# A transformer decoder layer on one core: the first attention fetch moved between queues, and the FFN's inner layernorm root computed by Newton's method on GpSimd

## The chip, the cores and the metric

The kernel runs on one core of a Trainium2 chip. The metric is the device time of one execution in microseconds (us); less is better. PE is TensorE, DVE is VectorE, ACT is ScalarE, POOL is GpSimd and SP is SyncE, which here only issues DMAs. PE, ACT, SP and POOL each have a queue in which instructions stand in order.

## The reference

One pre-norm decoder layer in fp32 for 4 batches of 1024 tokens with 256 features and 16 heads of 16 features, a context of 64 tokens, and an FFN of width 1024:

```
def _layernorm(x, eps=1e-05):
    return (x - mean(x)) / sqrt(var(x) + eps)

x = x + attn(_layernorm(x))            # softmax(q k^T) / 16 @ v, out projection
x = x + xattn(_layernorm(x), ctx)      # softmax(q k^T / 4) @ v over 64 context tokens
h = _layernorm(x) @ ternary(W_fc).T    # 256 -> 1024
h = gelu(h)
h = (h - mean(h)) * rsqrt(var(h) + 1e-05) * ln_w + ln_b      # the inner layernorm, over 1024
x = x + h @ ternary(W_proj).T          # 1024 -> 256
```

`ternary(W)` rounds W over its mean absolute value to -1, 0 or 1.

## The kernel before, in words

**Front, 0 to 63 us.** The first layernorm and the q and k projections of batch 0 run tile by tile. `project` (lines 360 to 376) computes two feature blocks of q or k for 512 tokens on PE into a bank of `ps_ring` (seven banks in turn), ACT copies it, rounded, to the first half of `hl` (line 370), DVE writes the remainder to its second half (line 371), and one DMA stores both to DRAM in `kept_q` or `kept_k` (line 376). Of the first feature block, the first store goes out on SP and the other three on ACT's queue. `fetch(u)` (lines 379 to 410) then brings the q and k of one group of four heads back into SBUF as small DMAs of 16 rows each, which lay the high and low parts of each head beside one another. A group has two pairs of heads, `pair` 0 and 1, and each pair two sides `n`, on partitions from 64n. Group 0 is fetched in halves of 512 columns so that it can start early: for each pair first q (first columns, line 401), then k (first and second columns, line 404), and at the end the second columns of q. Of k, the pieces of side `n` = 0 go out on ACT's queue and those of `n` = 1 on SP's.

**Groups, 63 to 1095 us.** There are 16 groups `u` (4 batches x 4 groups of 4 heads), each of 16 steps. Each step computes scores, their exponentials on ACT (line 909) and the weighted sum of values in `ps_acc`; meanwhile scores of the following half group go through PE once more and DVE takes their maxima `mx` (`maxima`, line 447), 32 for a half group of group 0 at the beginning. `turn_maxima` makes the negative maximum `nm` of them (line 456), without which the exponentials can't start. The order of all matmuls on PE is the order of the program. The other stages (next batch's projections, out projection, cross attention) are put between steps by credit lines.

**Tail, 1095 to 1355 us.** The FFN runs in eight halves of a batch, i = 0 to 7, each of four tiles of 128 tokens. `widen(i)` normalises x (line 265), transposes it on PE, writes it rounded to `xh` (ACT, line 279) with its remainder in `xl` (DVE, line 281), multiplies by `wfc`, takes Gelu (ACT, line 1029) and the statistics `mvh` of each tile (DVE, lines 1032 and 1033). It then takes the root through `ln_rstd` (lines 245 to 248): Sqrt on ACT into `sd`, reciprocal on DVE into `rsh`, then `nmr` = -mean * rsh on DVE (line 1037). With these the four tiles of h are normalised, two on DVE (line 1040), two on ACT (line 1043). `narrow(i)` transposes h on PE, writes it times `lnw` as `hT` (ACT, line 1063) with remainder `hl` (DVE, line 1064), and multiplies both by `wproj`; at the end x is completed and stored. Sqrt, Exp and Gelu lie in different activation tables of ACT, and a change between them is an ACT_TABLE_LOAD.

Each of the two is a generator, and the `yield`s cut it into pieces. A loop takes the next piece of whichever generator has the smallest place in a table:

```
WIDE, NARROW = (-6, -4, 0, 1, 3, 7, 8, 10, 12), (2, 4, 5, 6, 9, 11, 13, 14, 15)
wides = [Source(widen(i), 16 * i, WIDE) for i in range(halves)]
narrows = [Source(narrow(i), 16 * (i + 1), NARROW) for i in range(halves)]
```

So `narrow(i)` runs beside `widen(i + 1)`. In turns with `turn % 5 in (0, 2)` the loop takes a piece of the last batch's out projection and cross attention instead, as long as there are any; that work uses Exp (line 636). A piece of `widen` whose tag is Gelu or Sqrt is held back (`apart`) while a run of four Exp pieces is not complete. The program's order binds PE; on ACT and DVE a scheduler orders the instructions by what they need.

Of the kernel before, what the change touches and what calls it, by code (L numbers as in the profile page):

```python
# [8 lines left out]

F32 = mybir.dt.float32  # L10
F32R = mybir.dt.float32r
DRAM = bass.MemoryType.DRAM
AF = mybir.ActivationFunctionType
ALU = mybir.AluOpType
# [7 lines left out]
P = 128  # L22
NT = S // P
NG = 4
NU = B * NG
LN_EPS = 1e-5
# [4 lines left out]
def decoder_layer(ctx, tc, a, out):  # L31
# [15 lines left out]
    nc = tc.nc  # L47
# [54 lines left out]
    for name in ("wq", "wk"):  # L102
# [5 lines left out]
        t = const.tile([P, E // P, H, D], F32, name=name)  # L108
# [4 lines left out]
    for name in ("bq", "bk"):  # L113

        t = const.tile([P, 2], F32, name=f"{name}_c")
# [33 lines left out]
    own = post_pool.tile([P, 4], F32, name="own")  # L149
    sel_x = post_pool.tile([P, 8, SK], F32R, name="sel_x")  # L150

# [9 lines left out]
    for i in range(3):  # L161
        t = (const if i else main).tile([P, NT, VW], F32, tag=f"v_sb{i}", name=f"v_sb{i}")
# [81 lines left out]
    def ln_rstd(pool, rs, mv):  # L244
        n = mv.shape[1]
        sd = pool.tile([P, n], F32, tag="sd", name="sd", bufs=2)
        nc.scalar.activation(sd, mv[:, :, 1], AF.Sqrt, bias=eps_t[:, 0:1])
        pinned(nc.vector.reciprocal(out=rs, in_=sd))

    def ln_normalised(pool, mv, rs, i, t, n):  # L250
        xn = pool.tile([P, n, E], F32, tag="xn", name="xn", bufs=2)
        if state["split"]:
            nmr = pool.tile([P, n], F32, tag="nmr", name="nmr", bufs=2)
            nc.vector.scalar_tensor_tensor(
                nmr, mv[:, i : i + n, 0], -1.0, rs[:, i : i + n], ALU.mult, ALU.mult
            )
            for k in range(n):
                nc.scalar.activation(  # L258
                    xn[:, k, :], xs(t + k)[:, 0, :], AF.Identity, bias=nmr[:, k : k + 1],
                    scale=rs[:, i + k : i + k + 1],  # L260
                )
            return xn
        for k in range(n):
            pinned(
                nc.vector.tensor_scalar(
                    xn[:, k, :], xs(t + k)[:, 0, :], mv[:, i + k, 0:1], rs[:, i + k : i + k + 1],
                    ALU.subtract, ALU.mult,
                )
            )
        return xn  # L270
# [81 lines left out]
    def project(b, c):  # L352
# [6 lines left out]
        for side, half in ((0, 0), (1, 0), (1, 1), (0, 1)):  # L359
# [3 lines left out]
            for i0 in range(0, 512, width):  # L363
# [5 lines left out]
                )  # L369
                nc.scalar.activation(hl[:, 0, part].bitcast(F32R), pq, AF.Identity, bias=bias)  # L370
                nc.vector.scalar_tensor_tensor(  # L371
# [7 lines left out]
    def fetch(u):  # L379

        b, g = divmod(u, NG)
        pairs = qk_of[u] = []
        rest = []
        for pair in range(2):
            q = main.tile([P, S], F32R, tag="q", name="q", bufs=4)
            k = main.tile([P, S], F32R, tag="k", name="k", bufs=4)
            pairs.append((q, k))
            kept_q, kept_k = split_of[b, g // 2]
            f0 = 64 * (g % 2) + 32 * pair

            def parts(t, kept, order, n, cols, issue, f0=f0):
                for i, part in enumerate(order):
                    r, f = 64 * n + 16 * i, f0 + 16 * n
                    issue(out=t[r : r + 16, cols].bitcast(F32), in_=kept[part, f : f + 16, cols])

            if u:
                halves = (slice(0, S),)
            else:
                halves = (slice(0, 512), slice(512, S))
            for n in range(2):  # L400
                parts(q, kept_q, (0, 0, 1, 1), n, halves[0], dma)
            for cols in halves:
                for n in range(2):
                    parts(k, kept_k, (0, 1, 0, 1), n, cols, dma if u or n else nc.scalar.dma_start)
            for n in range(2):
                for cols in halves[1:]:
                    rest.append((parts, q, kept_q, (0, 0, 1, 1), n, cols, dma))
            if pair:
                for f, *args in rest:
                    f(*args)  # L410
            yield
# [42 lines left out]
    def turn_maxima(u, mx):  # L454
# [3 lines left out]
        dst = nm_s[:, :, :, 0:2, :]  # L458
        nc.vector.tensor_copy(dst[:, :, :, :, 0].bitcast(F32R), by_side)
        nc.vector.tensor_tensor(dst[:, :, :, :, 1], by_side, dst[:, :, :, :, 0], ALU.subtract)  # L460
        yield
        views = turned([nm_s[:, n, :, :, :].rearrange("p n a l -> p (n a l)") for n in range(4)])
        mT = main.tile([P, 512], F32R, tag="mT", name="mT", bufs=3)
        for r, v in enumerate(views):
# [237 lines left out]
    urgent, due, later, aside = deque(), Line(), Line(), Line()  # L702
# [132 lines left out]
    first, parts = ln1(0), project(0, 0)  # L835
# [35 lines left out]
    parts = project(0, 1)  # L871
# [40 lines left out]
    for u in range(NU):  # L912
# [27 lines left out]
        for step in range(2 * NT):  # L940
            half, kb = divmod(step, NT)
# [15 lines left out]
            exps = [scores(u, half, kb, 0)]  # L957
# [42 lines left out]
    ffn = ctx.enter_context(tc.tile_pool(name="ffn", bufs=1))  # L1000
    out_view = out.rearrange("(t p) d -> p t d", p=P)
    h_of = {}
    NH = NT // 2

    def widen(i):
        t0 = i * NH
        xh = ffn.tile([P, 2, NH * P], F32R, tag="xh", name="xh", bufs=2)
        xl = ffn.tile([P, 2, NH * P], F32R, tag="xl", name="xl", bufs=2)
        for t in range(0, NH, 2):
            cols = slice(t * P, (t + 2) * P)  # L1010
            xn = ln_normalised(ffn, mv3, rs3, t0 + t, t0 + t, 2)
            ln_transposed(xh[:, :, cols], xn, rest=xl[:, :, cols])
            if t == 0:
                yield ""
        h = ffn.tile([P, NH, HID], F32, tag="h", name="h", bufs=2)
        mv = ffn.tile([P, NH, 2], F32, tag="mvh", name="mvh", bufs=2)
        rs = ffn.tile([P, NH], F32, tag="rsh", name="rsh", bufs=2)
        h_of[i] = h
        for t in range(NH):
            yield "Gelu"  # L1020
            ph = ps["wide"]()
            for half in range(2):
                for k in range(4):
                    c, part = divmod(k, 2)
                    matmul(
                        ph[:, half, :], lhsT=(xl, xh)[part][:, c, t * P : (t + 1) * P],
                        rhs=wfc[:, c, half * 512 : (half + 1) * 512], start=k == 0, stop=k == 3,
                    )
            nc.scalar.activation(h[:, t, :], ph.rearrange("p a f -> p (a f)"), AF.Gelu)  # L1029
            st = ffn.tile([P, 2, 6], F32, tag="bnh", name="bnh", bufs=3)  # L1030
            for half in range(2):
                nc.vector.bn_stats(out=st[:, half, :], in_=h[:, t, half * 512 : (half + 1) * 512])  # L1032
            nc.vector.bn_aggr(out=mv[:, t, :], in_=st)
        yield "Sqrt"
        ln_rstd(ffn, rs, mv)
        nmr = ffn.tile([P, NH], F32, tag="nmr", name="nmr", bufs=2)
        nc.vector.scalar_tensor_tensor(nmr, mv[:, :, 0], -1.0, rs, ALU.mult, ALU.mult)
        for t in range(0, NH, 2):
            yield ""
            nc.vector.tensor_scalar(  # L1040
                h[:, t, :], h[:, t, :], mv[:, t, 0:1], rs[:, t : t + 1], ALU.subtract, ALU.mult
            )
            nc.scalar.activation(
                h[:, t + 1, :], h[:, t + 1, :], AF.Identity, bias=nmr[:, t + 1 : t + 2],
                scale=rs[:, t + 1 : t + 2],
            )
# [57 lines left out]

    WIDE, NARROW = (-6, -4, 0, 1, 3, 7, 8, 10, 12), (2, 4, 5, 6, 9, 11, 13, 14, 15)
    halves = 2 * B
    wides = [Source(widen(i), 16 * i, WIDE) for i in range(halves)]
    narrows = [Source(narrow(i), 16 * (i + 1), NARROW) for i in range(halves)]  # L1110
    exps = turn = 0
    tag = later.tag
    while tag is not None or narrows:
        turn += 1
        if tag is not None and turn % 5 in (0, 2):
            exps += "Exp" in tag
            tag = next(last, None)
            continue
        sources = []
        if wides:  # L1120
            i = halves - len(wides)
            first = len(wides[0].places) <= len(WIDE) - 2
            late_x = i >= 2 * (B - 1) and tag is not None
            full = first and len(narrows) > halves + 1 - i
            apart = exps % NG and tag is not None and wides[0].tag in ("Gelu", "Sqrt")
            if not (late_x or full or apart):
                sources.append(wides[0])
        if narrows and len(narrows) > len(wides):
            sources.append(narrows[0])
        if not sources:  # L1130
            continue
        source = min(sources, key=lambda source: source.places[0])
        source.step()
        if not source:
            (wides if source in wides else narrows).pop(0)
# [58 lines left out]
```

## Time and profile before

| | |
|---|---|
| median of 3 runs | 1352.89 us (1351.7 to 1353.23) |
| profiled execution | 1356.75 us |
| its span | 1355.0 us (1.75 us of the execution lie around it) |
| mean granted TensorE clock | 0.978 of full speed |
| PE busy | 1282.8 us, 95% of the span |
| DVE, ACT, POOL busy | 75%, 66%, 4% |
| ACT table loads | 15.4 us at line 1029, 24.4 us at line 247, 11.5 us at line 909, 3.8 us at line 636, each load 1.283 us |

The profile is of one execution, 3.86 us above the median. A timeline row gives the start, the duration, the engine, the line, the operation and its tiles, how many of them were run together (x2), and in brackets how long the engine stood idle before and what ended that. An engine with a q (ACTq, SPq) is issuing a DMA. The slices of the page cut the span into 40 equal parts of 33.9 us and show the busy share of each in tenths.

### The profile page before, as it was taken

How to read it: one execution, taken by the hardware profiler on the slowest of the kernel's cores; microseconds unless marked ns; L12 is line 12 of the kernel's file. 1: busy time of each engine (PE TensorE's matmuls, PEld its weight loads, DVE VectorE, ACT ScalarE, POOL GpSimd, SP SyncE). 2: the span in 40 equal slices, each digit the busy share in tenths (PEclk: the TensorE clock that was granted, in tenths of full speed). 3: DMA queues.
4: the chain of work that ended last, by engine and by line, in shares of the span. 5: the costliest groups of instructions: out<-in, count | busy, mean ns of one | idle time of the engine just before them, and what ended most of it. 6: DMA issues, size and time to landing. Idle time of an engine off the chain costs nothing.

```text
span 1355.0 us, 27659 instructions
## 1 busy us (share of the span) xinstructions
PE 1282.8 (95%) x11000; PEld 719.0 (53%) x11000; DVE 1013.4 (75%) x2130; ACT 896.3 (66%) x1654; POOL 53.4 (4%) x66
## 2 busy tenths in 40 slices
PE   4889999999999999989999999999999999999987
PEld 2344545545545454444545544545455457776777
DVE  5777877867878888778777777778888468585765
ACT  1267686756687767677676676676766756575755
POOL 4000000003010000011000000010000000000000
PEclk9789999999999999999999999999999999999989
DMA  5440412212120202030202111312110010100000
GB/s 165 134 126 29 129 37 90 79 48 63 39 89 1 63 5 60 32 94 25 71 30 66 28 36 53 105 40 87 41 55 1 1 63 1 59 4 32 1 32 31
DMA packets 46576, 72.72 MB, mean 54 GB/s; under 512 B 11536, under 2 KB 28176, under 8 KB 46448
## 3 DMA queue, kind: packets, MB, share of 16 engines
q1 hardware_dynamic: 44976, 68.47, 16.8%
q10 hardware_dynamic: 1328, 2.10, 0.5%
q8 instruction: 87, 1.43, 0.4%
q0 software_dynamic: 144, 0.39, 0.2%
q14 instruction: 41, 0.34, 0.1%
HBM read 46.81 MB, written 24.12 MB: 52 GB/s over the span
## 4 chain that ended last, share of the span: by engine, by line
PE 74%; DVE 16%; ACT 7%; DMA 2%; issue 1%; SPq 0%; DVEq 0%; ACTq 0%
PE ps_ring L57 43%; PE ps_acc L57 15%; PE ps_wide L57 8%; DVE mx L447 7%; PE ps_misc L57 3%; DVE nm L603 3%; ACT exp L909 2%; PE ps_misc L60 2%; PE ps_ring L60 2%; ACT xn L258 1%; DVE bn L241 1%; DMA kept_k<-hl 1%; DMA x<-in_x 1%; ACT ex L636 1%; SPq L63 0%
## 5 line engine op out<-in xcount | busy, mean ns | idle before, releaser
L447 DVE TENSOR_REDUCE mx<-ps_ring 128x1 f32<-128x512 f32 x1024 | 646.9, 682 | 157.5 <-PE ps_ring L57 156.8
L909 ACT ACTIVATE exp<-ps_ring 128x512 f32<-128x512 f32 x1024 | 549.1, 607 | 182.1 <-PE ps_ring L57 178.7
L57 PE MATMUL ps_ring<-q,k 64*128 64x512 f32 x1024 | 280.4, 475 | 6.5 <-ACT exp L909 5.6
L57 PE MATMUL ps_ring<-k,q 64*128 64x512 f32 x1024 | 266.5, 428 | 18.2 <-DMA k<-kept_k 6.6
L57 PE MATMUL ps_acc<-exp,v_sb 128*32 128x512 f32 x2048 | 275.3, 610 | 0.0
L57 PE MATMUL ps_ring<-mT,sel 64*128 64x512 f32 x1024 | 233.4, 402 | 0.4 <-ACT mT L465 0.4
L57 PEld LDWEIGHTS ps_ring<-q,k 64*128 64x128 f32 x1024 | 115.8, 186 | 198.1 <-ACT exp L909 65.7
L57 PEld LDWEIGHTS ps_ring<-k,q 64*128 64x128 f32 x1024 | 127.0, 187 | 100.6 <-ACT exp L909 41.8
L57 PEld LDWEIGHTS ps_ring<-mT,sel 64*128 64x128 f32 x1024 | 108.7, 187 | 6.5 <-ACT mT L465 0.7
L57 PEld LDWEIGHTS ps_acc<-exp,v_sb 128*32 128x32 f32 x2048 | 40.5, 108 | 67.8 <-issue 66.0
L1064 DVE SCALAR_TENSOR_TENSOR hl<-ps_misc,lnw,hT 128x512 fp32r<-128x512 f32 x64 | 46.6, 734 | 20.0 <-ACT hT L1063 19.8
L1032 DVE BATCH_NORM_STATS2 bnh<-h 128x6 f32<-128x512 f32 x64 | 41.1, 680 | 24.7 <-ACT h L1029 24.6
L57 PE MATMUL ps_wide<-wfc,xl 128*128 128x512 f32 x128 | 55.6, 435 | 3.6 <-DVE xl L281 3.1
L1029 ACT ACTIVATE h<-ps_wide 128x1024 f32<-128x1024 f32 x32 | 32.7, 1025 | 36.8 <-PE ps_wide L57 36.7
L57 PE MATMUL ps_wide<-wproj,hl 128*128 128x256 f32 x256 | 46.8, 306 | 10.6 <-DVE hl L1064 10.5
L1063 ACT ACTIVATE hT<-ps_misc,lnw 128x512 fp32r<-128x512 f32 x64 | 42.9, 687 | 15.3 <-PE ps_misc L60 15.2
L57 PE MATMUL ps_wide<-wfc,xh 128*128 128x512 f32 x128 | 52.9, 413 | 0.0
L241 DVE BATCH_NORM_STATS2 bn<-x 128x6 f32<-128x256 f32 x96 | 39.0, 416 | 5.8 <-DMA x<-in_x 4.1
L57 PEld LDWEIGHTS ps_wide<-wproj,hl 128*128 128x128 f32 x256 | 35.3, 194 | 14.3 <-DVE hl L1064 12.6
L57 PE MATMUL ps_wide<-wproj,hT 128*128 128x256 f32 x256 | 42.0, 287 | 0.0
L371 DVE SCALAR_TENSOR_TENSOR hl<-ps_ring,bq_c,hl 128x256 f32<-128x256 f32 (+1 forms) x30 | 14.8, 500 | 31.0 <-ACT hl L370 31.0
L60 PE MATMUL ps_misc<-ident,h 128*128 128x128 f32 x256 | 37.3, 275 | 0.0
(167 smaller groups left out, 1424.0 us busy)
## 6 DMA issues: line engine op xcount, KB each, us to landing
q<-kept_q SPq DMA_DIRECT2D x240, 64.0 KB
k<-kept_k SPq DMA_DIRECT2D x240, 64.0 KB
kept_q<-hl SPq DMA_DIRECT2D x15, 512.0 KB
kept_k<-hl SPq DMA_DIRECT2D x14, 512.0 KB
out<-x SPq DMA_DIRECT2D x16, 256.0 KB
x<-in_x SPq DMA_DIRECT2D x3, 1024.0 KB
x_kept<-x SPq DMA_DIRECT2D x3, 1024.0 KB
x<-x_kept SPq DMA_DIRECT2D x3, 1024.0 KB
```

The lines of the kernel that those rows point to most:

```text
L57: ordered(nc.tensor.matmul(*args, **kwargs))
L60: ordered(nc.tensor.transpose(*args))
L241: pinned(nc.vector.bn_stats(out=st, in_=xs(t)[:, 0, :]))
L258: nc.scalar.activation(xn[:, k, :], xs(t + k)[:, 0, :], AF.Identity, bias=nmr[:, k : k + 1], scale=rs[:, i + k : i + k + 1],)
L371: nc.vector.scalar_tensor_tensor(hl[:, 1, part], pq, bias, hl[:, 0, part], ALU.add, ALU.subtract)
L447: nc.vector.tensor_reduce(mx[:, t, 2 * pair + n : 2 * pair + n + 1, kh], pm, AX.X, ALU.max)
L603: nc.vector.tensor_reduce(nm[:, t, s, :], pm[s].rearrange("p (h k) -> p h k", k=SK), AX.X, ALU.max, negate=True,)
L909: nc.scalar.activation(ex[:, n, :], pe[n], AF.Exp)
L1029: nc.scalar.activation(h[:, t, :], ph.rearrange("p a f -> p (a f)"), AF.Gelu)
L1032: nc.vector.bn_stats(out=st[:, half, :], in_=h[:, t, half * 512 : (half + 1) * 512])
L1063: nc.scalar.activation(hT, pt, AF.Copy, scale=w)
L1064: nc.vector.scalar_tensor_tensor(hl, pt, w, hT.bitcast(F32), ALU.mult, ALU.subtract)
```

## The change

It does two things. First, `fetch(0)` issues nothing on ACT's queue any more: the k pieces of side 0 go to SP's queue for pair 0 (8 DMAs) and to GpSimd's queue for pair 1 (8 DMAs). Second, the FFN's inner layernorm takes its inverse root in `ln_root`, 17 GpSimd operations on 128x4 elements: a first value from the bits of the variance, three Newton steps, and `nmr`; the Sqrt on ACT and the reciprocal and `nmr` on DVE of this layernorm go. The yield with the tag Sqrt goes with them, so `widen` has one piece less. In the table the last two pieces of `widen`, which normalise h, stand at 12 and 13 instead of 10 and 12, and a piece of `narrow` stands at 8 that was at 13. The share of turns for the last batch goes from 2 of 5 (0.400) to 7 of 17 (0.412).

```diff
+I32 = mybir.dt.int32
...
+    def ln_root(pool, rs, mv):
+        n = mv.shape[1]
+        by = pool.tile([P, 4, n], F32, tag="root", name="root", bufs=2)
+        var, half, t, nmr = (by[:, i, :] for i in range(4))
+        engine = nc.gpsimd
+        engine.tensor_scalar(var, mv[:, :, 1], LN_EPS, None, ALU.add)
+        engine.tensor_scalar(half, var, -0.5, None, ALU.mult)
+        engine.tensor_scalar(
+            rs.bitcast(I32), var.bitcast(I32), -0.5, float(0x5F3759DF), ALU.mult, ALU.add
+        )
+        for _ in range(3):
+            engine.tensor_tensor(t, rs, half, ALU.mult)
+            engine.tensor_tensor(t, t, rs, ALU.mult)
+            engine.tensor_scalar(t, t, 1.5, None, ALU.add)
+            engine.tensor_tensor(rs, rs, t, ALU.mult)
+        engine.tensor_tensor(nmr, mv[:, :, 0], rs, ALU.mult)
+        engine.tensor_scalar(nmr, nmr, -1.0, None, ALU.mult)
+        return nmr
...
             for cols in halves:
                 for n in range(2):
-                    parts(k, kept_k, (0, 1, 0, 1), n, cols, dma if u or n else nc.scalar.dma_start)
+
+                    aside = u == 0 and pair == 1 and n == 0
+                    parts(k, kept_k, (0, 1, 0, 1), n, cols, nc.gpsimd.dma_start if aside else dma)
...
             nc.vector.bn_aggr(out=mv[:, t, :], in_=st)
-        yield "Sqrt"
-        ln_rstd(ffn, rs, mv)
-        nmr = ffn.tile([P, NH], F32, tag="nmr", name="nmr", bufs=2)
-        nc.vector.scalar_tensor_tensor(nmr, mv[:, :, 0], -1.0, rs, ALU.mult, ALU.mult)
+        nmr = ln_root(ffn, rs, mv)
...
-    WIDE, NARROW = (-6, -4, 0, 1, 3, 7, 8, 10, 12), (2, 4, 5, 6, 9, 11, 13, 14, 15)
+    WIDE, NARROW = (-6, -4, 0, 1, 3, 7, 12, 13), (2, 4, 5, 6, 8, 9, 11, 14, 15)
...
-        if tag is not None and turn % 5 in (0, 2):
+        if tag is not None and turn % 17 in (0, 2, 5, 7, 10, 12, 15):
...
-            apart = exps % NG and tag is not None and wides[0].tag in ("Gelu", "Sqrt")
+            apart = exps % NG and tag is not None and wides[0].tag == "Gelu"
```

## The prediction

> **What bounds the kernel now.** I read the page first: busy shares, slices, the chain that ended last; then the timeline of each engine where the slices are not full, and the windows there.
>
> ```profile
> span 1355.0 us, 27659 instructions
> PE 1282.8 (95%) x11000; PEld 719.0 (53%) x11000; DVE 1013.4 (75%) x2130; ACT 896.3 (66%) x1654; POOL 53.4 (4%) x66
> PE   4889999999999999989999999999999999999987
> POOL 4000000003010000011000000010000000000000
> PEclk9789999999999999999999999999999999999989
> ```
>
> PE is full except in the first three slices (34 us each) and the last two; Pool is empty. The change touches only those two ends, the attention steps between them shift as a block. So the question is how many us PE's stalls lose at each end.
>
> Front: the timeline of ACT, then of DVE, 24 to 64 us (columns: start, duration, engine, line, operation, count, idle before it).
>
> ```profile
> 25.82 2.39 ACTq L394 DMA_DIRECT2D k<-kept_k  x2
> 28.73 8.18 ACTq L394 DMA_DIRECT2D k<-kept_k  x13
> 37.01 0.84 ACT L370 ACTIVATE hl<-ps_ring,bq_c 128x256 fp32r<-128x256 f32 x2 [10.88 <-DMA q<-kept_q]
> 44.27 0.87 DVE L371 SCALAR_TENSOR_TENSOR hl<-ps_ring,bq_c,hl 128x256 f32<-128x256 f32 x2
> 45.06 0.87 DVE L371 SCALAR_TENSOR_TENSOR hl<-ps_ring,bk_c,hl 128x256 f32<-128x256 f32 x2
> 48.24 13.25 DVE L447 TENSOR_REDUCE mx<-ps_ring 128x1 f32<-128x512 f32 x22 [1.12 <-PE ps_ring L57]
> 61.52 0.19 DVE L456 TENSOR_REDUCE nm<-mx 128x16 f32<-128x32 f32 x1
> ```
>
> ACT issues the k fetches of group 0 until 36.9 us, so its four hl copies come at 37.0 instead of 26, DVE's partners of them at 44.3, and four of the seven ring banks stay taken. PE, which fills banks for the 32 maxima (mx), starves, and runs slowly too: the window 36 to 48 has a granted clock of 0.50. Only ten maxima are done before 48.24; the other 22 run back to back at 13.25/22 = 0.602 us; attention's first exponentials wait for nm at 61.5.
>
> Tail: one half of the FFN, 1284 to 1290 us, by the timeline; then the window around it (core's span, PE, PEld, DVE, ACT, POOL busy, clock).
>
> ```profile
> 1284.82 1.28 ACT L247 ACT_TABLE_LOAD   x1
> 1286.11 0.30 ACT L247 ACTIVATE sd<-mvh,eps_t 128x4 f32<-128x4 f32 x1
> 1286.44 0.18 DVE L248 RECIPROCAL rsh<-sd 128x4 f32<-128x4 f32 x1 [0.81 <-ACT sd L247]
> 1286.84 0.16 DVE L1037 SCALAR_TENSOR_TENSOR nmr<-mvh,rsh 128x4 f32<-128x4 f32 x1
> 1286.91 1.53 DVE L1040 TENSOR_SCALAR h<-h,mvh,rsh 128x1024 f32<-128x1024 f32 x2
> 1287.03 2.37 ACT L1043 ACTIVATE h<-h,nmr,rsh 128x1024 f32<-128x1024 f32 x2
> 1288.36 0.75 DVE L1064 SCALAR_TENSOR_TENSOR hl<-ps_misc,lnw,hT 128x512 fp32r<-128x512 f32 x1
> 1289.16 1.22 PE L57 MATMUL ps_wide<-wproj,hl 128*128 128x256 f32 x4 [2.70 <-DVE hl L1064]
> 1286.00:1296.00 10.00, 7.30 (x36) 6.22 (x36) 7.40 (x15) 6.22 (x8) 0.00 (x0) 0.83 0.15 52
> ```
>
> The root stands in the middle of ACT's and DVE's queues: PE waits for an hl that stands behind both normalisations. There are four such gaps: 1124.02 (2.92), 1233.50 (2.70; this one for two table loads between Exp and Gelu), 1289.16 (2.70), 1313.32 (2.90); 11.2 us, and PE then runs at half clock for 3.4 us (three times, 1.7 us lost) or 6.8 (the last, 3.4 lost), another 8.5. Gaps of up to 1.5 us (1336.77, 1263.07) are not followed by that.
>
> **Part 1: the first fetch.** In the changed program's order ACT issues no k piece; SP issues 16 k pieces after its first q pieces instead of 8, and Pool the other 8.
> - ACT's four hl follow at once: its kept_k store goes out at about 23.6 instead of 24.96 (before, it stands behind the first k issue, which waits for the first store), lands 4.03 later (24.96 to 28.99) at 27.7, and hl of both engines is done by about 27.5.
> - SP: 16 x 0.46 us (3.66/8) from 27.8 to 35.2. The first eight are the pieces needed first; they land, at 1.8 to 2.8 us, by 34.3. The second eight by 37.5. Then eight q of the second pair to 38.9, eight k to 42.6, sixteen q to 50.0. SP's old end of this is 48.7, so the stores behind it and fetch(1) come 1.3 us later; group 1's pieces, there by 70, are not used before the second half of group 0's steps (about 95), nor the x loaded behind them before 88, which hides it. If that cover were gone it would cost those 1.3.
> - Pool is idle after 20.7. Eight issues at 0.54 to 0.69 (its own rows bo, xbv) are 4.3 to 5.5 us, from about 27.8 to 33; landing at 5.7 to 6.2 (same rows) is 39. They are needed at the 17th maximum, about 44: covered by 5 us. Nothing else of Pool's is due then.
> - The maxima: from 33 us, the first eight at half clock for some 3.4 us (0.86 each) and then at 0.602, done by 40; the other 24 at 0.602 = 14.4: 54.5 to 55.5. nm comes at about 55 instead of 61.5. Gain 6.5; at an SP pace of 0.6 (the first three q have 3.69/3, with a wait in it) the first pieces land 3 us later and some 3 are left; bounds 2 and 8.
>
> **Part 2: the root on Pool.** Removed: 15 table loads (the changed order has 10 in the tail, before 25) at 1.283 = 19.2 us of ACT, 8 sd x 0.298 = 2.4, and of DVE 8 x (0.175 + 0.157) = 2.7. Neither is PE's time; it counts only through the gaps. A row says what stands behind a load: 1284.82 + 1.28 is 1286.10, and sd starts at 1286.11. The Trainium skill, "ScalarE: Activation LUTs", section "What ACT_TABLE_LOAD costs", adds a drain of about 1.38 us to each switch; that would make it 39.9 us of ACT instead of 19.2, but this trace shows no such drain.
>
> Added: 17 Pool operations of 128x4 in a chain (15 to rsh, 17 to nmr) for each half, each waiting for the one before. No 128x4 operation of Pool is in the trace. Below: memset 128x1, 0.10 us. Above: memset 64x32, 0.317. Nearest: copy 128x64 0.237 and 128x256 0.401, 0.85 ns an element, so 0.185 for four elements; two operands cost twice that per element (128x512 1.274 against 0.625), which is nothing at four. To it comes the hand-over, 0.03 to 0.05 (nm's three steps on DVE start 0.03 after one another; Pool shows 0.05). I take u = 0.23 a step, the copy row's; the bounds are 0.13 and 0.36, a step can't cost less than nothing, and the two rivals below stand just inside them, at 0.15 and 0.33. The chain is then 15u = 3.45 and 17u = 3.9 us, where load, sd, reciprocal and nmr take 2.2 (1284.82 to 1287.0), and ACT and DVE stand in order behind it: xh, xl, q and nm wait with it.
>
> Against this speaks the Trainium skill, "GPSIMD Engine Reference", section "4.1 Engine selection": elementwise work belongs on VectorE, about 2 times faster for two inputs. By a factor of two on DVE's 0.16 to 0.18 the step would be an estimated 0.34 and the change a loss; the copy row above says 0.185.
>
> Place by place, from the end of mvh's aggregation, with the durations above (normalisation DVE 1.53, ACT 2.37; xl 0.69; xh 0.57), gain of PE:
> - half 0: xl ready at 1117.55 + 15u + 1.53 + 0.69 + 0.1, against 1124.02: 4.15 - 15u.
> - half 1: q stands behind ACT's normalisation, PE would reach it 1.05 us after a root without duration: 1.05 - 17u (a new stall).
> - half 3: the Exp/Gelu gap goes (+3.1), DVE's nm of the cross attention waits behind the normalisation: 3.2 - 15u.
> - half 5 to 6: from the last wfc to the next 10.6 now (1280.45 to 1291.03), then 3.1 to mvh + 15u + 2.4: 5.1 - 15u.
> - half 6 to 7: 10.76 now, then 6.9 + 17u: 3.86 - 17u.
> - last: 7.78 now (1330.03 to 1337.81), then 5.6 + 17u, and the gap of 0.73 at 1340.02 goes: 2.9 - 17u.
> - halves 2 and 4: PE has other work; 0.
>
> Sum 20.3 - 96u. At 0.23: -1.8. Half-clock stretches: the one behind 1289.16 goes (+1.7), one comes in half 1 (-1.7), the others stay. Tail: -2. At 0.15: +5.9, and two or three stretches go, some +9. At 0.33: -11.4, with two or three new ones -15.
>
> **Sum.** 6.5 - 2 = 4.5 us less: the profiled execution of 1356.75 would be 1352.2. It stands 3.86 above the median of 1352.89, so the median becomes 1348.4.
>
> **Rivals.**
> - Slower: the Pool chain is the bound. At 0.33 a step, ACT and DVE wait 5 to 5.6 us in every half, PE falls to half clock behind it: 15 lost against 6.5 gained, 1361. It decides from u = 0.26 (with half clock) to 0.28. For it: 96 of these steps lie on the path, and a row of 0.317 exists. Against: the copy row.
> - The front's gain is lost: all of the first k pieces go through one queue, land late, and DVE waits as before: gain 1 to 2, with the tail 1353. For it: the first three q took 3.69. Against: 8 issues in 3.66 three times.
> - A cheap Pool step, 0.15: all four big gaps close, 6.5 + 9, 1337. For it: memset's 0.10. Against: that reads nothing.
>
> **Chances.** Forecast (u from 0.19 to 0.26, front whole) 0.42; Pool as bound 0.27; front lost 0.12; cheap step 0.19. The bound of 0.2% is 2.7 us, about what a measurement here can tell from no change. The cheap step and most of the forecast lie beyond it (0.54), the front lost and the forecast's upper u lie within (0.16), Pool as bound is slower (0.30 with the bad end of the lost front). The range runs from the cheap step, 1337, to the Pool bound, 1362.
>
> **What would show it.** Front: ACT's hl at 25 to 27, DVE's 22 or more continuous maxima from about 38 to 40, nm at 55, clock above 0.8 in 36 to 48. If nm is later than 59, part 1 is wrong. Tail: the mean of ln_root's rows and the distance of two (0.23); no gap over 2 us before the wfc of half 6; a new stall at kx,q in half 1 of about 2.9 and a longer one before the last transposes. A pace of 0.15 or 0.33 there makes the prediction wrong in the sense of the rival. If the pace is 0.23 and the tail still moves by over 4 us, my sum of places is wrong.

## The result and the profile after

The changed kernel takes 1371.96 us (median of 4, 1369.61 to 1373.83) against 1352.68 of the kernel before in the same runs: ratio 1.0135, 95% interval 1.0121 to 1.0148, so some 18 us slower (19 by the medians). The profiled execution takes 1372.11 us, its span is 1370.3.

The page of the changed kernel, busy shares and slices:

```profile
span 1370.3 us, 27791 instructions
PE 1285.3 (94%) x11000; PEld 721.4 (53%) x11000; DVE 1012.2 (74%) x2114; ACT 875.3 (64%) x1631; POOL 89.1 (7%) x210
PE   5889999999999999999999999999999988989887
POOL 5000000040100000011000000010000011110211
```

The last eight slices of PE were six 9s, an 8 and a 7; now they are two 9s, five 8s and a 7, and POOL is busy just there. Of 144 more POOL instructions 136 are the chains (17 in each of eight halves), 8 the fetch.

The front, by the timelines of DVE, SP and POOL:

```profile
37.60 18.03 DVE L472 TENSOR_REDUCE mx<-ps_ring 128x1 f32<-128x512 f32 x30 [1.90 <-PE ps_ring L58]
55.66 0.19 DVE L481 TENSOR_REDUCE nm<-mx 128x16 f32<-128x32 f32 x1
26.66 8.73 SPq L64 DMA_DIRECT2D k<-kept_k  x16
25.61 1.94 POOL L417 DMA_DIRECT2D k<-kept_k  x4 [4.63 <-DMA kept_k<-hl]
27.81 1.91 POOL L417 DMA_DIRECT2D k<-kept_k  x4 [0.26 <-DMA kept_k<-hl]
```

Thirty maxima run without a break from 37.6, where before it was 22 from 48.24, and nm comes at 55.66 instead of 61.52. The granted clock in 36 to 48 us is 0.92 instead of 0.50. The first transposes of the tail (oT) stand at 1091.37 instead of 1100.05. From there to the end it takes 278.9 us, against 255.0 before: 24 lost.

The change of half 6 to 7 in the tail, all engines (POOL's middle operations left out). This is the stretch for which the prediction had 3.86 - 17u:

```profile
1317.02 0.20 DVE L1058 BATCH_NORM_AGGREGATE mvh<-bnh 128x2 f32<-128x12 f32 x1
1317.38 0.23 POOL L259 TENSOR_SCALAR root<-mvh 128x4 f32<-128x4 f32 x1 [19.09 <-DVE mvh L1058]
...
1321.42 0.20 POOL L268 TENSOR_TENSOR rsh<-rsh,root 128x4 f32<-128x4 f32 x1
1321.69 0.20 POOL L269 TENSOR_TENSOR root<-mvh,rsh 128x4 f32<-128x4 f32 x1
1321.98 0.57 POOL L270 TENSOR_SCALAR root<-root 128x4 f32<-128x4 f32 x1
1321.65 1.53 DVE L1062 TENSOR_SCALAR h<-h,mvh,rsh 128x1024 f32<-128x1024 f32 x2 [2.84 <-POOL rsh L268]
1322.58 2.37 ACT L1065 ACTIVATE h<-h,root,rsh 128x1024 f32<-128x1024 f32 x2 [4.56 <-POOL root L270]
1324.86 1.05 ACT L302 CAST xh<-ps_misc 128x512 fp32r<-128x512 f32 x2
1325.45 1.29 DVE L304 TENSOR_TENSOR xl<-ps_misc,xh 128x512 fp32r<-128x512 f32 x2 [1.67 <-ACT xh L302]
1326.20 0.79 PE L58 MATMUL ps_wide<-wfc,xl 128*128 128x512 f32 x1 [5.06 <-DVE xl L304]
```

Read it from the bottom: PE stands 5.06 us for xl, xl waits for xh, xh stands in ACT's queue behind the normalisation, and that waits for the chain. From the end of mvh (1317.22) it is 4.40 us to rsh and 5.33 to nmr. The steps follow one another every 0.29 us, not 0.23: each takes 0.19 to 0.23, the hand-over to the next 0.06 to 0.10, and the last takes 0.57. In all eight halves together ACT stands idle for 31.8 us in front of this normalisation (the idle time behind the second bar of the group's line; 1.8 us in the kernel before):

```profile
L1065 ACT ACTIVATE h<-h,root,rsh 128x1024 f32<-128x1024 f32 x16 | 19.1, 1234 | 31.8 <-POOL root L270 31.8
```

Behind the gap PE runs at half clock; the window right after it (columns as before: length, PE, PEld, DVE, ACT, POOL, clock, DMA):

```profile
1326.20:1331.50 5.30, 5.30 (x13) 4.13 (x14) 1.56 (x3) 1.02 (x1) 0.00 (x0) 0.50 0.15 49
```

### The profile page after: what moved, and what is told of

Its sections match the earlier page's. It is cut to its first block, busy times and chain, and to the rows that moved or that the text cites. A ratio compares the mean times of both kernels' runs of the same rounds, so it can differ in the third digit from the quotient of the medians.

```text
span 1370.3 us, 27791 instructions
## 1 busy us (share of the span) xinstructions
PE 1285.3 (94%) x11000; PEld 721.4 (53%) x11000; DVE 1012.2 (74%) x2114; ACT 875.3 (64%) x1631; POOL 89.1 (7%) x210
## 3 DMA queue, kind: packets, MB, share of 16 engines
q8 instruction: 87, 1.43, 0.4%
## 4 chain that ended last, share of the span: by engine, by line
PE 71%; DVE 15%; ACT 7%; issue 2%; POOL 2%; DMA 1%; SPq 0%; POOLq 0%; DVEq 0%; ACTq 0%
PE ps_ring L58 43%; PE ps_acc L58 15%; DVE mx L472 7%; PE ps_wide L58 7%; ACT exp L934 2%; PE ps_misc L58 2%; PE ps_ring L61 2%; DVE nm L628 2%; PE ps_misc L61 2%; DVE bnh L1057 1%; ACT xn L281 1%; DMA x<-in_x 1%; ACT h L1054 1%; DVE hl L1086 1%; DVE bn L242 1%
## 5 line engine op out<-in xcount | busy, mean ns | idle before, releaser
L58 PE MATMUL ps_ring<-k,q 64*128 64x512 f32 x1024 | 263.7, 425 | 15.5 <-DMA k<-kept_k 6.0
L58 PE MATMUL ps_wide<-wfc,xl 128*128 128x512 f32 x128 | 58.2, 455 | 11.2 <-DVE xl L304 11.1
L1086 DVE SCALAR_TENSOR_TENSOR hl<-ps_misc,lnw,hT 128x512 fp32r<-128x512 f32 x64 | 46.6, 735 | 25.0 <-ACT hT L1085 24.8
L1065 ACT ACTIVATE h<-h,root,rsh 128x1024 f32<-128x1024 f32 x16 | 19.1, 1234 | 31.8 <-POOL root L270 31.8
```

What stands on the lines that cost most here:

```text
L58: ordered(nc.tensor.matmul(*args, **kwargs))
L1065: nc.scalar.activation(h[:, t + 1, :], h[:, t + 1, :], AF.Identity, bias=nmr[:, t + 1 : t + 2], scale=rs[:, t + 1 : t + 2],)
L1086: nc.vector.scalar_tensor_tensor(hl, pt, w, hT.bitcast(F32), ALU.mult, ALU.subtract)
```

## The experiments

**Theories.** L: the fetch gains, and the chain on GpSimd, 17 steps long, loses by its length in each of eight halves. O: the fetch gains, and the new places of the pieces lose it, whatever takes the root.

**Each part alone.** `front_only` is the kernel before with the changed lines of `fetch`; `tail_only` is the changed kernel with the old ones:

```diff
-                    aside = u == 0 and pair == 1 and n == 0
-                    parts(k, kept_k, (0, 1, 0, 1), n, cols, nc.gpsimd.dma_start if aside else dma)
+                    parts(k, kept_k, (0, 1, 0, 1), n, cols, dma if u or n else nc.scalar.dma_start)
```

> The kernel before with only the changed first fetch; the root stays on ACT with its old places. In the changed kernel's trace the tail begins 8.7 us earlier (1091.37 against 1100.05 for the same oT transposes). Theory L (the fetch gains, the 17-step chain on GpSimd loses it all) and theory O (the fetch gains, the new places of the pieces lose it) both expect 1352.7 - 8.7 = 1344, span about 1346. If the 8.7 also hold a lucky phase of PE's half-clock stretches in group 0 (nm was only 5.9 earlier), 1347.

> The changed kernel with the old first fetch. Both theories: the tail took 24 us more in the changed kernel's trace, so 1352.7 + 24 = 1377. If the two parts hinder or help one another (the phase of the half-clock stretches carries from the one to the other), it differs from that by more than 3.

`front_only`: 1348.4 us, ratio 0.9965 (0.9952 to 0.9977): 4.7 us gained, not 8.7. `tail_only`: 1378.15, ratio 1.0188 (1.0167 to 1.0208), 25 lost, as expected. The fetch's own gain is what nm shows: 55.39 here, 55.66 in the changed kernel, 6 earlier. What the changed kernel's trace had beyond it stands in group 0: from PE's stall at about 87 us to the next oT transposes it takes 13.34 us in `front_only` (87.75 to 101.09), 13.41 in the kernel before, but 11.49 in the changed kernel (87.23 to 98.72). The stall is 4.4 us long in all three; the clock is then 0.50 for 10.2 us in the first two (87.6 to 97.9, and 94.0 to 104.2 in the kernel before), and for 6.8 us in the changed kernel (85.8 to 92.6). The single executions of `front_only` lie from 1345.83 to 1352.37.

**The root back on ACT, the rest as changed** (`sqrt_new_places`):

```diff
-        nmr = ln_root(ffn, rs, mv)
+        ln_rstd(ffn, rs, mv)
+        nmr = ffn.tile([P, NH], F32, tag="nmr", name="nmr", bufs=2)
+        nc.vector.scalar_tensor_tensor(nmr, mv[:, :, 0], -1.0, rs, ALU.mult, ALU.mult)
```

> The changed kernel with fetch and new places kept, but the root again by Sqrt on ACT with reciprocal and nmr on DVE (no yield of its own). Theory L: the time from mvh to nmr falls from 5.4 us to about 2 to 2.5, the loads come back: 1344 to 1350. Theory O: the places cost it, so it stays near the changed kernel, 1365 to 1372.

1341.47 us, ratio 0.9919 (0.9900 to 0.9939): 11 us faster than the kernel before. Theory O falls: the new places gain. Beside `front_only` they (with the yield for Sqrt gone and the share of turns changed) are worth 0.9965 - 0.9919 = 0.0046, 6 us. And the chain in place of Sqrt alone costs 1.0135 - 0.9919 = 0.0216, 29 us. The same change of halves in this kernel:

```profile
1295.58 1.28 ACT L248 ACT_TABLE_LOAD   x1
1295.95 0.20 DVE L1058 BATCH_NORM_AGGREGATE mvh<-bnh 128x2 f32<-128x12 f32 x1
1296.88 0.30 ACT L248 ACTIVATE sd<-mvh,eps_t 128x4 f32<-128x4 f32 x1
1297.21 0.18 DVE L249 RECIPROCAL rsh<-sd 128x4 f32<-128x4 f32 x1 [0.44 <-ACT sd L248]
1297.42 0.16 DVE L1061 SCALAR_TENSOR_TENSOR nmr<-mvh,rsh 128x4 f32<-128x4 f32 x1
1301.62 0.50 PE L58 MATMUL ps_wide<-wfc,xl 128*128 128x512 f32 x1 [1.38 <-DVE xl L304]
```

The load starts before mvh is ready (1295.58 against 1296.15), so from mvh it is here 1.24 us to rsh and 1.43 to nmr: 3.2 and 3.9 less than through GpSimd. Not every half is so short: from mvh to nmr it is 0.74 to 2.92 us in the eight halves, 2.06 on the mean, against 5.43 through GpSimd. The load starts before mvh is ready in five of the eight, and in the half shown 0.71 of its 1.28 us still lie behind mvh. PE's gap is 1.38 instead of 5.06, and no half clock follows it (clock of 1301.62 to 1305: 1.00).

The tails of the profiled executions, from the first oT transposes to the end of the span, by windows:

| kernel | tail | PE busy | PE idle | clock |
|---|---|---|---|---|
| before | 255.0 | 230.6 | 24.4 | 0.96 |
| changed | 278.9 | 239.4 | 39.6 | 0.94 |
| `sqrt_new_places` | 247.2 | 224.5 | 22.7 | 1.00 |
| `pool_old_places` | 288.9 | 246.9 | 42.1 | 0.90 |
| `norm_late` | 288.8 | 242.3 | 46.6 | 0.92 |
| `one_newton_step` | 261.0 | 231.0 | 30.0 | 0.96 |
| `five_newton_steps` | 293.5 | 246.9 | 46.6 | 0.90 |
| `dve_two_steps` | 244.6 | 227.1 | 17.6 | 0.99 |

PE's instructions are the same 1440 in each, so more busy time is PE at half clock. Between the changed kernel and `sqrt_new_places` 16.9 us are gaps and 14.9 the half clock behind them. Eight times the 3.4 us between 5.43 and 2.06 is 27, but that it lies near the 29 is no check of the price, since half of the difference is half clock.

**The chain with the old places** (`pool_old_places`; the tables before, less one place of `widen`, and `turn % 5 in (0, 2)`):

```diff
-    WIDE, NARROW = (-6, -4, 0, 1, 3, 7, 12, 13), (2, 4, 5, 6, 8, 9, 11, 14, 15)
+    WIDE, NARROW = (-6, -4, 0, 1, 3, 7, 10, 12), (2, 4, 5, 6, 9, 11, 13, 14, 15)
```

> The changed kernel (new fetch, three Newton steps on GpSimd) with the places of the kernel before: normalisation at 10 and 12, the piece of narrow at 13, 2 of 5 turns for the last batch. Theory L: the chain costs some 3.2 us more than Sqrt in each of eight halves here too, so with the fetch's gain of 5 about 1348 + 20 to 26 = 1368 to 1374; the places do not make the loss. If the loss came from chain and new places together, nearer to 1350.

1381.26 us, ratio 1.0209 (1.0192 to 1.0226). The chain costs 1.0209 - 0.9965 = 0.0244, 33 us, with the old places, and the new ones take 10 of that back. The expected time was too low, the direction is theory L's.

**The normalisation later** (`norm_late`: the two pieces with the normalisation go from the end of `widen` into the first piece of `narrow`, WIDE ends at 7):

```diff
         nmr = ln_root(ffn, rs, mv)
-        for t in range(0, NH, 2):
-            yield ""
...
+        h_of[i] = h, mv, rs, nmr
...
-        h = h_of.pop(i)
+        h, mv, rs, nmr = h_of.pop(i)
+        for t in range(0, NH, 2):
...
```

> The changed kernel with the chain on GpSimd as long as it is, but the normalisation of h is written at the start of narrow, after the next half's xh and xl, instead of at the end of widen. Theory L in its form that the in-order queues of ACT and DVE hold xh, xl and q behind a normalisation that waits for the chain: the stalls before wfc (3.17, 2.71, 5.06 us) and before kx,q (2.56) go for the most part, 1372 - 8 to 12 = 1360 to 1364, with the wait before the last transposes unchanged (about 3 us). If only the chain's length counts, wherever the normalisation stands (PE then waits for h instead of for xl), it stays at 1370 to 1374.

1381.63 us, ratio 1.0211 (1.0196 to 1.0226), 10 slower than the changed kernel and outside both expected ranges. The gaps before wfc shrink (no such gap of over 2.2 us is left), but PE then stands for h itself:

```profile
1283.16 0.21 DVE L1057 BATCH_NORM_AGGREGATE mvh<-bnh 128x2 f32<-128x12 f32 x1
1287.80 1.53 DVE L1066 TENSOR_SCALAR h<-h,mvh,rsh 128x1024 f32<-128x1024 f32 x2 [4.43 <-POOL rsh L268]
1288.75 0.45 PE L61 MATMUL ps_misc<-ident,h 128*128 128x128 f32 x1 [7.95 <-DVE h L1066]
```

Of these 7.95 us 2.6 lie before mvh is ready (1283.37), the rest is the chain and the first normalisation. So this edit doesn't take the wait for the chain away, it moves it from xl to h; DVE and ACT also stand longer in front of the normalisation (27.1 and 39.1 us in the tail instead of 22.7 and 31.8). The run doesn't tell the chain's length from what its wait holds up.

**The length of the chain** (`one_newton_step`, `five_newton_steps`: `range(1)` and `range(5)` for `range(3)`, 9 and 25 operations for 17):

> The changed kernel with one Newton step on GpSimd instead of three: 9 operations instead of 17 (the root is less exact). Theory L: from mvh to nmr 0.25 + 9 x 0.29 + 0.3 = 3.1 us instead of 5.4, so on the line between Sqrt in the new places (2.2 us, 1341.5) and the changed kernel (5.4 us, 1371): about 1350. Rival H: not the length but the handing to and from GpSimd and the half clock behind any wait that is left cost it, whatever the length: 1362 or more.

> The changed kernel with five Newton steps: 25 operations. Theory L: mvh to nmr 7.8 us, 9 us for each us more of it (the line of the two runs: 30 us for 3.2 us): 1372 + 21 = 1393. The scheduler puts the normalisation behind xh in two more halves here, which by theory L in its in-order form takes some of that back: 1380 to 1393. Rival H: 1372 to 1376.

1355.38 us, ratio 1.0007 (0.9996 to 1.0019), and 1385.1, ratio 1.0231 (1.0204 to 1.0258). Rival H falls: 9, 17 and 25 operations lie 1, 18 and 31 us over the kernel before, 2.2 and then 1.6 us an operation, or 0.27 and 0.20 in each of eight halves, by steps of 0.29. One step came out 5 us slower than said: there ACT normalises before the next half's xh in half 0, and a gap of 3.24 us before wfc stays; and in half 2 DVE's normalisation, which waits for the chain, stands in front of attx, so that PE waits 5.30 us for attx (at 1189.53) where it waits 2.29 in the changed kernel.

**The root on DVE** (`dve_three_steps`, `dve_two_steps`; with two operations fused where DVE can, 13 and 10 operations; the edit with two steps):

```diff
+        dve.tensor_scalar(var, mv[:, :, 1], LN_EPS, None, ALU.add)
+        dve.tensor_scalar(
+            rs.bitcast(I32), var.bitcast(I32), -0.5, float(0x5F3759DF), ALU.mult, ALU.add
+        )
+        dve.tensor_scalar(mhalf, var, -0.5, None, ALU.mult)
+        for _ in range(2):
+            dve.tensor_tensor(t, rs, rs, ALU.mult)
+            dve.tensor_tensor(t, t, mhalf, ALU.mult)
+            dve.scalar_tensor_tensor(rs, t, 1.5, rs, ALU.add, ALU.mult)
+        dve.scalar_tensor_tensor(nmr, mv[:, :, 0], -1.0, rs, ALU.mult, ALU.mult)
```

> The changed kernel with the same three Newton steps on DVE, two operations fused into one where DVE can: 13 operations of 128x4, at 0.21 us a step (nm's three steps on DVE) 2.7 us from mvh to nmr, no table loads. Theory L: 1341.5 + 0.5 x 9 = 1346, less what the missing loads are worth (Sqrt in the new places had 10 more loads): 1340 to 1346. If DVE's queue is the bound in the tail, its 13 x 0.21 x 8 = 22 us of occupation cost more: 1355.

> As the run with three steps on DVE, with two: 10 operations, 2.1 us from mvh to nmr. Theory L: 3 to 5 us less than with three steps, 1337 to 1342; as fast as Sqrt in the new places or a little faster.

1346.41 us, ratio 0.9943 (0.9924 to 0.9963), and 1338.44, ratio 0.9880 (0.9865 to 0.9895): the second is the fastest of all, 16 us under the kernel before. Part of one chain on DVE:

```profile
1295.02 0.15 DVE L1069 TENSOR_TENSOR root<-rsh 128x4 f32<-128x4 f32 x1
1295.20 0.16 DVE L1070 TENSOR_TENSOR root<-root 128x4 f32<-128x4 f32 x1
1295.39 0.16 DVE L1071 SCALAR_TENSOR_TENSOR rsh<-root,rsh 128x4 f32<-128x4 f32 x1
1295.59 0.17 DVE L1069 TENSOR_TENSOR root<-rsh 128x4 f32<-128x4 f32 x1
1295.73 0.69 DVE L304 TENSOR_TENSOR xl<-ps_misc,xh 128x512 fp32r<-128x512 f32 x1
```

A step every 0.19 us, 0.15 to 0.17 of it work; and between steps DVE takes xl, which in the changed kernel waits behind the chain. The executions with three steps spread from 1341.53 to 1352.53, those with two from 1337.34 to 1340.04; the granted clock of the ten with three goes from 0.990 at the fastest to 0.980 at the slowest. A hundredth of 1345 us is 13, so half clock is enough for the spread; why some executions have more of it stays open.

Both times lie where theory L put them or within 1 us of it, but not for its reason. The way from mvh to nmr was to be 2.7 and 2.1 us; it is 4.7 and 3.7, because of the other work between the steps. From the profiled executions, tail only:

| kernel | mvh to nmr, mean of eight | DVE idle just before it normalises h, us in all | ACT idle there | execution |
|---|---|---|---|---|
| `sqrt_new_places` | 2.06 | 0.0 | 1.0 | 1341.01 |
| `dve_two_steps` | 3.69 | 0.0 | 7.6 | 1338.76 |
| `dve_three_steps` | 4.73 | 0.0 | 10.3 | 1341.53 |
| `one_newton_step` | 3.04 | 11.1 | 20.3 | 1354.87 |
| changed | 5.43 | 22.7 | 31.8 | 1372.11 |
| `five_newton_steps` | 7.88 | 35.8 | 46.8 | 1391.07 |

Nine operations on GpSimd are through sooner than ten or thirteen on DVE, and the kernel is still 9 and 17 us slower by the medians. So the time from mvh to nmr alone is not the price. The times go rather with how long DVE and ACT stand idle in front of the normalisation, with xh, xl, q and attx behind it: the three rows in which DVE doesn't stand idle lie within 3 us, and with GpSimd's chain both idle times grow with its operations. This is read across runs; no run changes the idle time alone.

**One operation fewer on DVE** (`dve_short`):

> The run with two steps on DVE with one operation less (first value from the variance without eps, half by one fused operation): 9 operations of 128x4. Theory L: 0.2 us less in each half, at most 1.7 us: 1336 to 1338.5; where DVE fills the chain's gaps with other work anyway, no difference.

1340.35 us, ratio 0.9913 (0.9892 to 0.9934): no gain over two steps, as in the second case of the expectation. An effect of the 1.7 us at most that were expected would be within the spread of the executions (1339.42 to 1344.86).

**GpSimd's last operation** (`norm_waits_for_nmr`):

```diff
-                h[:, t, :], h[:, t, :], mv[:, t, 0:1], rs[:, t : t + 1], ALU.subtract, ALU.mult
+                h[:, t, :], h[:, t, :], rs[:, t : t + 1], nmr[:, t : t + 1], ALU.mult, ALU.add
```

> The changed kernel, with DVE's normalisation written as h times rsh plus nmr, so that it starts after the chain's last operation and not beside it. Theory P (GpSimd's last operation takes 0.56 us instead of 0.23 because DVE's 128x1024 normalisation reads and writes SBUF at the same time): its mean falls to about 0.23, and ACT's normalisation starts 0.3 us earlier after the chain's beginning. If the operation is long for itself (the first use of the scalar -1.0, say), it stays at 0.56. The time: DVE starts 0.4 us later in each half and ACT 0.3 earlier, 1368 to 1374.

The groups of the changed kernel, then of this one:

```profile
L270 POOL TENSOR_SCALAR root<-root 128x4 f32<-128x4 f32 x8 | 4.5, 565 | 0.7
```

```profile
L270 POOL TENSOR_SCALAR root<-root 128x4 f32<-128x4 f32 x8 | 1.8, 226 | 0.7
```

Theory P holds: 565 ns beside DVE's normalisation, 226 without it. The Trainium skill, "GPSIMD Engine Reference", section "8. Key points", says that GpSimd shares its SBUF interfaces with VectorE and collides with some DVE instructions; this pair of rows agrees. The time of its one execution is 1372.86 us, which can't be told from the changed kernel's.

**The fetch without GpSimd's queue** (`fetch_sp_only`: the kernel before, all k pieces by `dma`):

> The kernel before with all k pieces of group 0 on SyncE's queue, none on ACT's and none on GpSimd's. If freeing ACT is what gains: nm at 55 to 57, 1348 to 1350 as with the changed fetch, since the second pair's pieces are then issued by 46.5 and land by 49, and wanted from about 44: up to 2 us of it lost. If GpSimd's queue is what makes it fast: nm at 59 or later, 1352 or more.

1347.93 us, ratio 0.9961 (0.9946 to 0.9975), the same as with GpSimd's queue. The maxima of this kernel:

```profile
35.93 9.66 DVE L447 TENSOR_REDUCE mx<-ps_ring 128x1 f32<-128x512 f32 x16 [1.90 <-PE ps_ring L57]
46.82 8.46 DVE L447 TENSOR_REDUCE mx<-ps_ring 128x1 f32<-128x512 f32 x14 [1.24 <-PE ps_ring L57]
55.31 0.19 DVE L456 TENSOR_REDUCE nm<-mx 128x16 f32<-128x32 f32 x1
```

The second pair's pieces come 1.24 us late, and nm is still at 55.31. It is ACT's freedom that gains; of a gain by the third queue nothing is seen.

## Why the prediction was wrong

**Part 1 held.** nm at 55 was forecast, it is at 55.66; SP issued the first 16 k pieces in 8.73 us where 7.4 was forecast, the next sixteen pieces at the forecast 0.46 each, and its end came at 51.5 instead of 50.0; the GpSimd issues took 0.49 each. Of the 6.5 us forecast `front_only` shows 4.7 (3.1 to 6.5 by its interval); the GpSimd queue that the forecast gave a part has none in it.

**The step that failed is the price of the chain on GpSimd, twice.** The tail was forecast 2 us slower and came 24 slower. Of the 22 between, some 7 are the chain's own pace, 8.8 half clock, and 6 idle time of PE in places that were put at nothing.

First u: 0.23 was taken from one copy row and a hand-over of 0.03 to 0.05. The work of a step was about right (0.185 taken, 0.19 to 0.23 measured), the hand-over was 0.06 to 0.10, the first step starts 0.08 to 0.25 after mvh, and the last collides with DVE, 0.34 more. Over the whole chain that is 5.33 us to nmr in place of 3.9, or 0.31 a step. The sum 20.3 - 96u gives -9.5 with it, not -1.8 (-8.8 when each place takes the measured 4.4 to rsh or 5.3 to nmr). The bounds of 0.13 to 0.36 held it, and the rival that counted with 0.33 names the mechanism that the runs showed: ACT and DVE wait, and PE falls to half clock. Its loss of 15 us was still 9 too small.

Second, the half clock, put at nothing (one stretch goes, one comes). PE's busy time in the tail rose by 8.8 us (230.6 to 239.4) with the same instructions. The kernel before has four stretches in its tail in which the clock is 0.50, three of 3.4 us and one of 6.8, at its four gaps of 2.70 us or more. The changed kernel has eight, six of 3.4 and two of 6.8, one at every gap of over 2 us: 3.17, 2.06, 2.56 (with 1.58 behind it), 2.29, 2.07 (with 1.23), 2.71, 5.06 and 2.37 (with 0.96). No length of a gap that decides can be read from these runs: gaps of 2.30 and 2.03 in `sqrt_new_places` and one of 2.75 in `one_newton_step` (at 1289.50) were not followed by half clock, one of 1.82 in the latter (at 1312.29) was, and so were four short gaps of 0.16 to 0.69 us, 1.9 in all, in `dve_short` (up to 1326.17). The Trainium skill, "TensorE: Matmul & The Clock Gate", Part 1, tells of a free-running window of 3413 ns. A stretch of 3.4 us behind a gap of 2.92 and one of 6.8 behind a gap of 2.90 in the kernel before, and the 10.2 and 6.8 us at the 4.4 us stall of group 0 in `front_only` and the changed kernel, agree with a phase that the gap doesn't set.

**The places were right where they were priced.** With the measured 4.4 and 5.3, half 0 gives 4.15 - 4.4 = -0.25 (its gap went from 2.92 to 3.17), half 1 gives 1.05 - 5.3 = -4.3 (gaps of 2.56 and 1.58), half 3 gives 3.2 - 4.4 = -1.2 (2.70 before, 2.07 and 1.23 now), half 5 to 6 gives 5.1 - 4.4 = +0.7 (from wfc to wfc 10.55 before, 9.77 now), half 6 to 7 gives 3.86 - 5.3 = -1.5 (from wfc to wfc 10.77 and 12.13), the last 2.9 - 5.3 = -2.4 (gaps of 2.24 and 4.0). What was put at 0 elsewhere was not 0: gaps of 2.06 (1129.34) and 2.29 (1192.13) are new. The second stands in `sqrt_new_places` too (2.30) and not in `pool_old_places`, so it belongs to the new places; the first stands in both (1.66, and 2.06 at 1131.39), so what makes it stays open. PE's idle time rose by 15.2 us where the priced places give 8.8 with the measured chain; 6 us were missed elsewhere.

**The new places themselves were not priced.** The forecast took them with the chain, in one sum. `sqrt_new_places` shows them worth 6 us with Sqrt and `pool_old_places` 10 with the chain. The change's loss is thus 29 us of chain against 6 of places and 5 of fetch.

**The table loads.** That their 19.2 us on ACT count only through the gaps held: in `sqrt_new_places` the load starts before mvh is ready in five of eight halves, and Sqrt with 2.06 us from mvh to nmr on the mean beats any chain on GpSimd tried here. Of the rule that spoke against the change (elementwise work on VectorE) the direction holds, the factor of two doesn't at this size: a 128x4 operation takes 0.19 to 0.23 us on GpSimd and 0.15 to 0.17 on DVE, a step of the chain 0.29 against 0.19.

## What to carry to other kernels

Price a chain of small operations by its spacing, not by the operation, start and last step included, and set it against what the old path costs from the same event: of a table load only what is left when its input is ready counts there (0.71 of 1.28 us in the half shown). Ask which queues stand idle meanwhile: that, and not the chain's length alone, went with the time here. Multiply by every half in which PE has nothing else to do, and give PE's half clock a term of its own, which here was nearly as large as the gaps; the shortest gap that brings it could not be read from these runs. Where an edit moves work and moves it in the order too, price the two apart: here the order gained, and the fastest version is the new order with the chain on DVE, which can do other work between steps.

## What the runs showed of the hardware that was not expected

A GpSimd operation of 128x4 takes 0.19 to 0.23 us, and 0.56 when it falls together with DVE's 128x1024 tensor_scalar; also 0.56 and 0.58 beside a DVE add of two SBUF operands (line 314, at 1137.21 and 1138.41). DMA issues of 16 rows cost GpSimd's queue 0.49 us each, about SP's 0.46, and no difference to the kernel's time is seen between the two queues. Half clock follows gaps of PE as short as 1.8 and 2.1 us in some places and doesn't follow one of 2.75 in another.
